# A selective-scan layer: the products with C on GpSimd, half of the B scalings on ScalarE, state copies on VectorE

## The chip, the core and the metric

The kernel runs on one core of a Trainium2 chip. A core has five engines that run side by side, each in its own program order: TensorE (PE in the profile, with its weight loads as PEld), VectorE (DVE), ScalarE (ACT), GpSimd (POOL) and SyncE (SP), which issues most DMAs. Engines wait for each other by semaphores. [...] The metric is the device time of one execution in microseconds (us), lower being better: 5,275.88 us as the median of three runs (5,275.79 to 5,280.46).

## The reference

The network has four layers on a tensor of 2 x 256 x 48 x 48, that is 2 images of 2,304 tokens with 256 channels. Only layer 0 is touched here, a Mamba layer that runs once forward ("f") and once backward ("b") over the tokens. Its core, for each of 512 inner channels d and 16 states n, is

```
xs   = silu(causal_conv(xi) + conv_b)              # 4 taps
proj = xs @ xproj_w.T                              # 16 for dt, 16 for B, 16 for C
dt   = softplus(proj[:16] @ dtproj_w.T + dtproj_b)
A    = -exp(A_log)
h[t] = exp(dt[t] * A) * h[t-1] + (dt[t] * xs[t]) * B[t]     # scan over t
y[t] = sum over n of h[t] * C[t]  +  xs[t] * D
out  = x + ((y_f * silu(z) + y_b * silu(z)) @ out_proj_w.T)
```

The other layers (a convolution with linear attention, an attention with a routed feed-forward, and an attention with a mixture of experts) come after it and are the same in both kernels.

## The kernel before

Layer 0 is the function `layer0`. The tokens are cut into 6 chunks of W = 384, so with 2 images and 2 directions there are 24 pieces (`order`). A sequence is the 6 pieces of one image and direction; `step` is the chunk's number in it. All data is 32-bit floating point, with channels on the 128 partitions, so 512 inner channels make DB = 4 blocks, and a chunk makes TB = 3 blocks of 128 tokens.

A piece is a loop over 16 states n and, inside, 4 channel blocks d: 64 slots, called `TILES`, with slot number k. A slot handles one tile of 128 channels by 384 tokens:

- `decay` (L601): ScalarE computes he = exp(dt * A) for slot k + EXP_AHEAD (4), into one of 6 buffers.
- `scale_b` (L591): GpSimd multiplies dt * xs, which lies transposed (tokens on partitions, `dtt`), by the B of state n, one value per partition. There are three instructions of 128x512 for each state, two states ahead, into one of 3 `dbt` buffers.
- `turn_b` (L611): TensorE transposes these back into PSUM (`db`, 3 buffers), DB_AHEAD = 2 slots ahead.
- the scan (L744 forward, L746 backward): one VectorE instruction over the 384 tokens.
- the product with C (`cc`, broadcast over the partitions by DMA). For three states of four (`on_pool`) two scans write to SBUF (`ho`, 4 buffers), and GpSimd multiplies both at once (L753, 128x768, `hcp`, 7 buffers). For the fourth state (n % 4 == 3, slots 12 to 15, 28 to 31, 44 to 47, 60 to 63) the scan writes over `db` in PSUM, and VectorE multiplies (L760, 128x384, `hc`).
- the state after the chunk's last token, which starts the scan of the next piece, is copied by ScalarE (L755 for a pair, L762 for one) in all but the last piece of a sequence.
- `add_state` (L637): TensorE transposes the product and adds it up in PSUM over the states (`y`), POOL_LAG (10) or DVE_LAG (2) slots later, from the list `later`.

Between these, each slot leaves TensorE room for about one more matmul. `advance` fills it from generators, by how far each lags behind its line: `prepare` makes the next piece's inputs (convolution L319, x products L338, dt products L355, softplus, the dt-u product on GpSimd L377, its transposes L387) and is to be done by slot READY = 54; `project_in`, `project_out` and parts of later layers share the other way. Each way has one PSUM bank, which ScalarE or VectorE must empty before TensorE's next step. `begin` opens a piece's `y` in slots 8 to 10, `end` empties the last piece's in slot 7. SBUF buffers come from pools by tag; the layers are recorded through a scheduler that sets waits and may move instructions of an engine past others that are not ready.

Of the kernel before, what the change touches and what calls it, by code (L numbers as in the profile page):

```python
# [18 lines left out]
F32 = mybir.dt.float32  # L19
# [144 lines left out]
def layer0(ctx, E):  # L164
# [7 lines left out]
    EXP_AHEAD, DB_AHEAD, POOL_LAG, DVE_LAG = 4, 2, 10, 2  # L172
# [105 lines left out]
    for s in "fb":  # L278
        w_x[s] = big.tile([P, DB, 48], F32, name=f"w_x{s}")
        nc.sync.dma_start(w_x[s], p[f"xproj_wT_{s}"].rearrange("(k p) m -> p k m", p=P))  # L280
        w_dt[s] = big.tile([16, 512], F32, name=f"w_dt{s}")
        nc.sync.dma_start(w_dt[s], p[f"dtproj_wT_{s}"])
        nega[s] = big.tile([P, DB * NS], F32, name=f"nega{s}")
        nc.scalar.activation(nega[s], E.v(f"A_log_{s}"), AF.Exp)
        nc.vector.tensor_scalar(nega[s], nega[s], -1.0, None, ALU.mult)

        w_d[s] = big.tile([P, DB, P], F32, name=f"w_d{s}")
        for d in range(DB):
            nc.vector.tensor_scalar(w_d[s][:, d, :], E.ident, E.v(f"D_{s}", d, 1), None, ALU.mult)
# [15 lines left out]
    def prepare(b, s, step, c, got):  # L305
# [37 lines left out]
        pr = wp.tile([48, W], F32, tag="pr", name="pr")  # L343
        nc.scalar.copy(pr, pj[:48, :])
# [7 lines left out]
        bt = wp.tile([P, TB, 48], F32, tag="bt", name="bt")  # L352
# [12 lines left out]
        nc.vector.tensor_copy(bt.rearrange("p j n -> p (j n)"), pb[:, : TB * 48])  # L365
# [12 lines left out]
        yield 0  # L378
        yield 0
        yield 0  # L380
        yield 0
        yield 0
# [10 lines left out]
    N_PREPARE = 43  # L393
# [191 lines left out]
    def scale_b(g, j):  # L585

        if g * DB < last:
            pc, n, _ = at_piece(g * DB)
            if j == 0:
                dbt[g] = wp.tile([P, TB, D], F32, tag="dbt", name="dbt", bufs=3)  # L590
            nc.gpsimd.tensor_scalar(  # L591
                dbt[g][:, j, :], pc["dtt"][:, j, :], pc["bt"][:, j, 16 + n : 17 + n], 1.0,
                ALU.mult, ALU.mult,
            )
# [99 lines left out]
    for i in range(len(order)):  # L694
# [26 lines left out]
        if i + 1 < len(order):  # L721
            ways[0].append([prepare(*order[i + 1], made), N_PREPARE, 20 if i == 0 else 0, READY, 0])
        for n in range(NS):
            g = i * NS + n
            on_pool = n % 4 != 3
# [3 lines left out]
            for d in range(DB):  # L729
# [19 lines left out]
                end_at = W - 1 if fwd else 0  # L749
                if on_pool:  # L750
                    if d % 2:
                        hc = wp.tile([P, 2, W], F32, tag="hcp", name="hcp", bufs=7)
                        nc.gpsimd.tensor_tensor(hc, ho, bc(cc, [P, 2, W], 1), ALU.mult)  # L753
                        if step < NCH - 1:
                            nc.scalar.copy(state[:, n, d - 1 : d + 1], ho[:, :, end_at])  # L755
                        for e in range(2):
                            later.append((k + POOL_LAG + e, add_state, (pc, d - 1 + e, hc[:, e, :])))
                else:
                    hc = wp.tile([P, W], F32, tag="hc", name="hc", bufs=3)
                    nc.vector.tensor_tensor(hc, to, cc, ALU.mult)  # L760
                    if step < NCH - 1:
                        nc.scalar.copy(state[:, n, d : d + 1], to[:, end_at : end_at + 1])  # L762
                    later.append((k + DVE_LAG, add_state, (pc, d, hc)))
# [10 lines left out]
        later.append((k0 + TILES + 7, end, (pc,)))  # L774
# [1529 lines left out]
```

## Time and profile before

| what | value |
|---|---|
| timed median of three | 5,275.88 us |
| the profiled execution's own time | 5,228.29 us |
| its span, first to last instruction | 5,226.4 us |
| PE busy | 4,808.4 us, 92% |
| VectorE busy | 3,288.2 us, 63% |
| ScalarE busy | 2,406.3 us, 46% |
| GpSimd busy | 2,435.5 us, 47% |
| granted TensorE clock | 0.968 |

An engine's busy time is the sum of its instructions' spans. TensorE's matmuls overlap, so that its busy share is too high as a measure of use. The page cuts the span into 40 equal slices of 131 us; the Mamba layer is the part in which GpSimd is busy. A group of instructions is named by its source line, engine and operation, then what it writes and reads, then the count; after the bar come its busy time in us, the mean of one in ns, and the idle time of the engine just before such instructions with what ended it. A view of stretches gives the same busy times for any interval.

### The profile page before, as it was taken

Reading aid. Unit: us, or ns where it says so; the run is one execution under the profiler, and the core shown is the slowest. Engines: PE = TensorE matmul, PEld = TensorE weight load, DVE = VectorE, ACT = ScalarE, POOL = GpSimd, SP = SyncE. Lnnn points to the kernel's source line nnn. Section 1 sums busy time; section 2 is a strip of 40 time slices with the busy share of each in tenths; the row PEclk is TensorE's granted clock in tenths of the full one; section 3 lists DMA queues with packets and bytes.
Section 4 is the critical chain, followed back from the end, with each engine's and each line's share of the span. In section 5 each row is a group of like instructions: output and inputs, shape, how many; then the busy total and the mean of one; then the engine's idle time right before and its main releaser. Section 6 shows DMA issues by size and latency. Waiting matters only on the chain. (4 is left out here: it accounts for less than half of the span.)

```text
span 5226.4 us, 61396 instructions
## 1 busy us (share of the span) xinstructions
PE 4808.4 (92%) x22242; PEld 3138.2 (60%) x22242; DVE 3288.2 (63%) x4801; ACT 2406.3 (46%) x4600; POOL 2435.5 (47%) x2091
## 2 busy tenths in 40 slices
PE   7888899899899889888999999999999999999897
PEld 4666666666666666665555555556655555555675
DVE  4888888888887878888999445456725400212344
ACT  5767767776667667662223223322133222222221
POOL 4798888888898888883000000048512100000321
PEclk8999999999999999999999999999989999999999
DMA  3222222222211122213110000111121100000423
GB/s 98 79 74 78 81 78 87 89 84 83 83 63 56 55 70 86 77 61 112 39 45 29 7 16 1 42 34 28 16 97 49 49 6 6 7 10 9 85 83 99
DMA packets 156377, 294.16 MB, mean 56 GB/s; under 512 B 29495, under 2 KB 108347, under 8 KB 155804
## 3 DMA queue, kind: packets, MB, share of 16 engines
q1 hardware_dynamic: 147356, 277.37, 15.5%
q0 software_dynamic: 8704, 12.73, 1.6%
q8 instruction: 179, 2.93, 0.2%
q14 instruction: 138, 1.13, 0.1%
HBM read 211.97 MB, written 78.07 MB: 55 GB/s over the span
## 5 line engine op out<-in xcount | busy, mean ns | idle before, releaser
L753 POOL TENSOR_TENSOR hcp<-ho,cc 128x768 f32<-128x768 f32 x576 | 1078.6, 1874 | 175.4 <-DVE ho L744 88.1
L591 POOL TENSOR_SCALAR dbt<-dtt,bt 128x512 f32<-128x512 f32 x1152 | 860.1, 764 | 147.1 <-PE db L611 141.8
L611 PE MATMUL db<-ident,dbt 128*128 128x128 f32 x4608 | 794.8, 283 | 101.3 <-DVE ho L744 32.1
L611 PEld LDWEIGHTS db<-ident,dbt 128*128 128x128 f32 x4608 | 565.0, 144 | 463.9 <-issue 187.4
L637 PE MATMUL y<-ident,hcp 128*128 128x128 f32 x3456 | 577.4, 276 | 6.1 <-POOL hcp L753 6.1
L601 ACT ACTIVATE he<-dt,negab 128x384 f32<-128x384 f32 x768 | 461.4, 613 | 186.1 <-DVE ho L746 108.0
L601 ACT ACTIVATE he<-dt,negaf 128x384 f32<-128x384 f32 x768 | 463.3, 614 | 177.0 <-DVE ho L744 124.1
L744 DVE TENSOR_TENSOR_SCAN ho<-he,state,db 128x384 f32<-128x384 f32 x480 | 464.9, 1002 | 121.2 <-PE db L611 108.2
L746 DVE TENSOR_TENSOR_SCAN ho<-he,state,db 128x384 f32<-128x384 f32 x480 | 467.9, 1002 | 110.8 <-PE db L611 94.8
L637 PEld LDWEIGHTS y<-ident,hcp 128*128 128x128 f32 x3456 | 421.3, 143 | 29.9 <-issue 20.9
L2107 POOL DMA_INDIRECT xe<-xt_d,token x48 | 47.5, 990 | 753.9 <-issue 713.2
L319 PE MATMUL mm<-xw,w_cv 128*128 128x384 f32 x768 | 312.7, 494 | 37.2 <-ACT xs L329 24.6
L2042 PE MATMUL po<-at,xtok 128*128 128x384 f32 x864 | 329.5, 506 | 8.2 <-ACT at L2040 8.1
L2040 ACT ACTIVATE at<-sp 128x384 f32<-128x384 f32 x216 | 104.8, 491 | 467.2 <-PE sp L2033 467.1
L2033 PE MATMUL sp<-qT,xn 128*128 128x384 f32 x864 | 317.2, 486 | 0.0
L1680 PE MATMUL ph<-xn,w 128*128 128x384 f32 x768 | 286.0, 515 | 17.7 <-ACT hid L1684 7.0
L1238 POOL PARTITION_ALL_REDUCE most<-most x1 | 0.4, 422 | 621.0 <-DVE most L1237 621.0
L969 PE MATMUL pf<-t,wfc 128*128 128x384 f32 x768 | 254.9, 487 | 3.0 <-ACT hid L973 2.9
L2042 PEld LDWEIGHTS po<-at,xtok 128*128 128x128 f32 x864 | 149.8, 189 | 177.4 <-ACT at L2040 108.4
L988 PE MATMUL po<-hid,wfc 128*128 128x384 f32 x768 | 253.6, 486 | 0.0
L1684 ACT ACTIVATE hid<-ph,vec 128x384 f32<-128x384 f32 x192 | 110.6, 581 | 290.2 <-PE ph L1680 256.6
L2033 PEld LDWEIGHTS sp<-qT,xn 128*128 128x128 f32 x864 | 161.6, 190 | 105.2
(481 smaller groups left out, 8791.0 us busy)
## 6 DMA issues: line engine op xcount, KB each, us to landing
cc<-bcd SPq DMA_DIRECT2D x96, 768.0 KB, 4.0
xw<-xi_d SPq DMA_DIRECT2D x24, 774.0 KB, 4.6
w<-in_m_w SPq DMA_DIRECT2D x16, 1024.0 KB, 5.5
y_d<-y SPq DMA_DIRECT2D x32, 384.0 KB, 2.3
ye<-y_d SPq DMA_DIRECT2D x32, 384.0 KB, 3.1
xi_d<-xz SPq DMA_DIRECT2D x48, 192.0 KB, 1.9
z_d<-xz SPq DMA_DIRECT2D x36, 256.0 KB, 2.3
y<-z_d SPq DMA_DIRECT2D x12, 768.0 KB, 4.1
```

The costliest lines, as they stand in the source:

```text
L319: nc.tensor.matmul(px, lhsT=w_cv[b, s][:, d * 4 + k, :], rhs=xw[:, d, o : o + W], start=k == 0, stop=k == 3,)
L591: nc.gpsimd.tensor_scalar(dbt[g][:, j, :], pc["dtt"][:, j, :], pc["bt"][:, j, 16 + n : 17 + n], 1.0, ALU.mult, ALU.mult,)
L601: nc.scalar.activation(hes[k], pc["dt"][:, d, :], AF.Exp, scale=nega[pc["s"]][:, d * NS + n : d * NS + n + 1])
L611: nc.tensor.transpose(dbs[k][:, j * P : (j + 1) * P], dbt[k // DB][:, j, d * P : (d + 1) * P], E.ident)
L637: nc.tensor.matmul(pc["yt"][j][:, d * P : (d + 1) * P], lhsT=hc[:, j * P : (j + 1) * P], rhs=E.ident, is_transpose=True, start=False, stop ...
L744: nc.vector.tensor_tensor_scan(to, he, db, init, ALU.mult, ALU.add)
L746: nc.vector.tensor_tensor_scan(to[:, ::-1], he[:, ::-1], db[:, ::-1], init, ALU.mult, ALU.add)
L753: nc.gpsimd.tensor_tensor(hc, ho, bc(cc, [P, 2, W], 1), ALU.mult)
L969: nc.tensor.matmul(pf, lhsT=wfc1[:, k, f * P : (f + 1) * P], rhs=t1[:, k, :], start=k == 0, stop=k == 1,)
L1680: nc.tensor.matmul(ph, lhsT=w1[:, e, k, f * P : (f + 1) * P], rhs=xn[:, k, c * W : (c + 1) * W], start=k == 0, stop=k == 1,)
L2033: nc.tensor.matmul(sp, lhsT=xn[:, k, t0 + i * P : t0 + (i + 1) * P], rhs=qT[:, k, c * W : (c + 1) * W], start=k == 0, stop=k == 1,)
L2042: nc.tensor.matmul(po[m], lhsT=xtok[:, i, m * P : (m + 1) * P], rhs=at, start=i == 0, stop=i == MT - 1,)
```

## The change

- Every state's scans go in pairs to `ho`, and every product with C is made by GpSimd, 128x768; the VectorE path and its buffers are gone, with one LAG of 10.
- Of the three scalings by B of a state, ScalarE makes the first, and for odd n the second too; GpSimd makes the rest.
- The state is copied by VectorE, two blocks at a time.
- Exps go 6 ahead in place of 4, with 8 buffers in place of 6.
- The weights of the x products and dt products are widened with zeros or neighbouring columns, so that these matmuls use all 128 rows and columns; the transposes of the projection are then 128 wide, and only the 16 columns of B are copied out.
- `prepare` is to be done by slot 48, with 8 empty steps in place of 5 between the dt-u product and its transposes; `begin`, `end` and `project_out` move by some slots.

```diff
-    EXP_AHEAD, DB_AHEAD, POOL_LAG, DVE_LAG = 4, 2, 10, 2
+    NX = 3 * NS
+    EXP_AHEAD, DB_AHEAD, LAG = 6, 2, 10
...
-        w_x[s] = big.tile([P, DB, 48], F32, name=f"w_x{s}")
+        w_x[s] = big.tile([P, DB * NX + P - NX], F32, name=f"w_x{s}")
+        nc.vector.memset(w_x[s][:, DB * NX :], 0.0)
...
-        w_dt[s] = big.tile([16, 512], F32, name=f"w_dt{s}")
-        nc.sync.dma_start(w_dt[s], p[f"dtproj_wT_{s}"])
+        w_dt[s] = big.tile([P, D], F32, name=f"w_dt{s}")
+        nc.vector.memset(w_dt[s], 0.0)
+        nc.sync.dma_start(w_dt[s][0:NS, :], p[f"dtproj_wT_{s}"])
...
-                pj[:48, :], lhsT=w_x[s][:, d, :], rhs=xs[:, d, :], start=d == 0, stop=d == DB - 1
+                pj, lhsT=w_x[s][:, d * NX : d * NX + P], rhs=xs[:, d, :], start=d == 0, stop=d == DB - 1
...
-                pd, lhsT=w_dt[s][:, d * P : (d + 1) * P], rhs=pr[0:16, :], start=True, stop=True
+                pd, lhsT=w_dt[s][:, d * P : (d + 1) * P], rhs=pr, start=True, stop=True
...
-            nc.tensor.transpose(pb[:, j * 48 : (j + 1) * 48], pr[:, j * P : (j + 1) * P], E.ident[0:48, 0:48])
-        nc.vector.tensor_copy(bt.rearrange("p j n -> p (j n)"), pb[:, : TB * 48])
+            nc.tensor.transpose(pb[:, j * P : (j + 1) * P], pr[:, j * P : (j + 1) * P], E.ident)
+        nc.vector.tensor_copy(bt, pb.rearrange("p (j n) -> p j n", j=DB)[:, :TB, NS : 2 * NS])
...
-        yield 0
-        yield 0
-        yield 0
-        yield 0
-        yield 0
+        for _ in range(8):
+            yield 0
...
-    N_PREPARE = 43
+    N_PREPARE = 46
...
-            nc.gpsimd.tensor_scalar(
-                dbt[g][:, j, :], pc["dtt"][:, j, :], pc["bt"][:, j, 16 + n : 17 + n], 1.0,
-                ALU.mult, ALU.mult,
-            )
+            to, at, b_n = dbt[g][:, j, :], pc["dtt"][:, j, :], pc["bt"][:, j, n : n + 1]
+            if j == 0 or j == 1 and n % 2:
+                nc.scalar.activation(to, at, AF.Copy, scale=b_n)
+            else:
+                nc.gpsimd.tensor_scalar(to, at, b_n, 1.0, ALU.mult, ALU.mult)
...
-            hes[k] = wp.tile([P, W], F32, tag="he", name="he", bufs=6)
+            hes[k] = wp.tile([P, W], F32, tag="he", name="he", bufs=8)
...
-            later.append((k0 + 8 + j, begin, (pc, j)))
+            later.append((k0 + LAG + 1 + j, begin, (pc, j)))
...
-        at = 8
+        at = LAG + 1
         if after:
-            ways[1].append([after, N_OUT, at, at + 18, 0])
-            at += 19
+            ways[1].append([after, N_OUT, at, at + 12, 0])
+            at += 13
...
-            ways[0].append([prepare(*order[i + 1], made), N_PREPARE, 20 if i == 0 else 0, READY, 0])
+            ways[0].append([prepare(*order[i + 1], made), N_PREPARE, 20 if i == 0 else 0, READY - 6, 0])
...
-                if on_pool:
-                    if d % 2 == 0:
-                        ho = wp.tile([P, 2, W], F32, tag="ho", name="ho", bufs=4)
-                    to = ho[:, d % 2, :]
-                else:
-                    to = db
+                if d % 2 == 0:
+                    ho = wp.tile([P, 2, W], F32, tag="ho", name="ho", bufs=4)
+                to = ho[:, d % 2, :]
...
-                        if step < NCH - 1:
-                            nc.scalar.copy(state[:, n, d - 1 : d + 1], ho[:, :, end_at])
-                        for e in range(2):
-                            later.append((k + POOL_LAG + e, add_state, (pc, d - 1 + e, hc[:, e, :])))
-                else:
-                    hc = wp.tile([P, W], F32, tag="hc", name="hc", bufs=3)
-                    nc.vector.tensor_tensor(hc, to, cc, ALU.mult)
+                if d % 2:
+                    hc = wp.tile([P, 2, W], F32, tag="hcp", name="hcp", bufs=7)
+                    nc.gpsimd.tensor_tensor(hc, ho, bc(cc, [P, 2, W], 1), ALU.mult)
                     if step < NCH - 1:
-                        nc.scalar.copy(state[:, n, d : d + 1], to[:, end_at : end_at + 1])
-                    later.append((k + DVE_LAG, add_state, (pc, d, hc)))
+                        nc.vector.tensor_copy(state[:, n, d - 1 : d + 1], ho[:, :, W - 1 if fwd else 0])
+                    for e in range(2):
+                        later.append((max(k + e, k0 + 3) + LAG, add_state, (pc, d - 1 + e, hc[:, e, :])))
...
-        later.append((k0 + TILES + 7, end, (pc,)))
+        later.append((k0 + TILES + LAG + 1, end, (pc,)))
```

More of the change, by code (lines that the diff above doesn't have):

```diff
@@ L278, in layer0 @@
     for s in "fb":
-        w_x[s] = big.tile([P, DB, 48], F32, name=f"w_x{s}")
-        nc.sync.dma_start(w_x[s], p[f"xproj_wT_{s}"].rearrange("(k p) m -> p k m", p=P))
-        w_dt[s] = big.tile([16, 512], F32, name=f"w_dt{s}")
-        nc.sync.dma_start(w_dt[s], p[f"dtproj_wT_{s}"])
+        w_x[s] = big.tile([P, DB * NX + P - NX], F32, name=f"w_x{s}")
+        nc.vector.memset(w_x[s][:, DB * NX :], 0.0)
+        nc.sync.dma_start(
+            w_x[s][:, : DB * NX].rearrange("p (k m) -> p k m", k=DB),
+            p[f"xproj_wT_{s}"].rearrange("(k p) m -> p k m", p=P),
+        )
+        w_dt[s] = big.tile([P, D], F32, name=f"w_dt{s}")
+        nc.vector.memset(w_dt[s], 0.0)
+        nc.sync.dma_start(w_dt[s][0:NS, :], p[f"dtproj_wT_{s}"])
         nega[s] = big.tile([P, DB * NS], F32, name=f"nega{s}")
@@ L342, in prepare @@
                 yield 1
-        pr = wp.tile([48, W], F32, tag="pr", name="pr")
-        nc.scalar.copy(pr, pj[:48, :])
+        pr = wp.tile([P, W], F32, tag="pr", name="pr")
+        nc.scalar.copy(pr, pj)
         bcd = dr.tile([NS, W], F32, tag="bcd", name="bcd")
@@ L351, in prepare @@
         ex = up.tile([P, DB, W], F32, tag="ex", name="ex")
-        bt = wp.tile([P, TB, 48], F32, tag="bt", name="bt")
+        bt = wp.tile([P, TB, NS], F32, tag="bt", name="bt")
         for d in range(DB):
@@ L721, in layer0 @@
         if i + 1 < len(order):
-            ways[0].append([prepare(*order[i + 1], made), N_PREPARE, 20 if i == 0 else 0, READY, 0])
+            ways[0].append([prepare(*order[i + 1], made), N_PREPARE, 20 if i == 0 else 0, READY - 6, 0])
         for n in range(NS):
             g = i * NS + n
-            on_pool = n % 4 != 3
             if n % 4 == 0:
@@ L748, in layer0 @@
                     )
[L749 to L753, printed above, removed]
-                        if step < NCH - 1:
-                            nc.scalar.copy(state[:, n, d - 1 : d + 1], ho[:, :, end_at])
-                        for e in range(2):
-                            later.append((k + POOL_LAG + e, add_state, (pc, d - 1 + e, hc[:, e, :])))
-                else:
-                    hc = wp.tile([P, W], F32, tag="hc", name="hc", bufs=3)
-                    nc.vector.tensor_tensor(hc, to, cc, ALU.mult)
+                if d % 2:
+                    hc = wp.tile([P, 2, W], F32, tag="hcp", name="hcp", bufs=7)
+                    nc.gpsimd.tensor_tensor(hc, ho, bc(cc, [P, 2, W], 1), ALU.mult)
                     if step < NCH - 1:
-                        nc.scalar.copy(state[:, n, d : d + 1], to[:, end_at : end_at + 1])
-                    later.append((k + DVE_LAG, add_state, (pc, d, hc)))
+                        nc.vector.tensor_copy(state[:, n, d - 1 : d + 1], ho[:, :, W - 1 if fwd else 0])
+                    for e in range(2):
+                        later.append((max(k + e, k0 + 3) + LAG, add_state, (pc, d - 1 + e, hc[:, e, :])))
                 later.sort(key=lambda e: e[0])
```

## The prediction

> **What bounds the kernel now.** I read the page's slices first: GpSimd (POOL) is busy only in the first 19 of 40, so the Mamba layer, the only thing that changes, is the first 2,402 us. Then that stretch, from the first scan to the last, in the view of stretches (columns: length, then busy us of PE, PEld, DVE, ACT, POOL, then granted clock, DMA share, GB/s):
>
> ```profile
> 79.20:2402.00 2322.80, 2055.64 (x12465) 1502.93 (x12464) 1921.42 (x2196) 1612.71 (x3261) 1982.62 (x1749) 0.97 0.22 76
> ```
>
> It holds 24 pieces of 64 slots (one scan each), 96.8 us a piece. No engine is alone at its limit: VectorE is idle 401 us, GpSimd 340, ScalarE 710. PE's 2,056 overstates it, since its pipelined rows overlap. So I cut one ordinary piece at its scans 0, 8, 32, 40, 48 and 64 and read the same columns:
>
> ```profile
> 1632.10:1641.90 9.80, 9.80 (x65) 7.61 (x66) 7.83 (x10) 5.31 (x14) 9.80 (x11) 1.00 0.19 80
> 1641.90:1678.70 36.80, 34.67 (x211) 24.78 (x210) 27.57 (x32) 26.15 (x58) 31.76 (x32) 1.00 0.22 77
> 1678.70:1691.60 12.90, 12.85 (x79) 8.72 (x77) 8.36 (x10) 12.09 (x28) 9.12 (x9) 1.00 0.16 61
> 1691.60:1711.50 19.90, 15.07 (x65) 9.44 (x65) 16.46 (x17) 15.92 (x36) 18.19 (x12) 0.83 0.08 21
> 1711.50:1728.30 16.80, 14.26 (x115) 12.23 (x114) 16.75 (x23) 11.96 (x29) 14.85 (x14) 1.00 0.13 48
> ```
>
> The first stretch fills GpSimd; the middle two fill PE, with ScalarE at 94% in slots 32-40; slots 40-48 hold the end of the next piece's preparation, PE half idle and its clock at 0.83; the last 16 slots fill VectorE (16.75 of 16.80). An instruction more on VectorE costs time there, and is hidden in the middle. The rows that the change touches (line, engine, operation, count | busy us, mean ns | idle before, releaser):
>
> ```profile
> L760 DVE TENSOR_TENSOR hc<-db,cc 128x384 f32<-128x384 f32 x384 | 202.1, 545 | 6.2 <-PE y L637 2.0
> L755 ACT COPY state<-ho 128x2 f32<-128x2 f32 x480 | 91.3, 190 | 183.5 <-DVE ho L746 100.5 <-DVE ho L744 79.3 <-DVE ub L467 1.1
> L753 POOL TENSOR_TENSOR hcp<-ho,cc 128x768 f32<-128x768 f32 x576 | 1078.6, 1874 | 175.4 <-DVE ho L744 88.1 <-DVE ho L746 84.3 <-PE db L611 1.6
> L591 POOL TENSOR_SCALAR dbt<-dtt,bt 128x512 f32<-128x512 f32 x1152 | 860.1, 764 | 147.1 <-PE db L611 141.8 <-ACT dtt L388 2.4 <-ACT state L762 1.5
> L387 PE MATMUL mm<-ident,dtu 128*128 128x128 f32 x288 | 61.5, 354 | 59.8 <-POOL dtu L377 59.7
> ```
>
> What decides is how a small VectorE instruction fares beside a running GpSimd one. VectorE's and GpSimd's lines of the timeline (start, length):
>
> ```profile
> 1377.29 1.81 POOL L753 TENSOR_TENSOR hcp<-ho,cc 128x768 f32<-128x768 f32 x1
> 1377.98 1.14 DVE L485 TENSOR_TENSOR off<-gn 128x2 f32<-128x2 f32 x1
> 1379.07 0.70 POOL L591 TENSOR_SCALAR dbt<-dtt,bt 128x512 f32<-128x512 f32 x1
> 1379.15 0.64 DVE L486 TENSOR_SCALAR off<-off 128x2 f32<-128x2 f32 x1
> ...
> 1408.69 1.04 DVE L468 TENSOR_TENSOR ub<-ub,vec 128x1 f32<-128x1 f32 x1
> ```
>
> L485 moves two elements and lasts until 1379.12, where the product of 1377.29 ends (1379.10); L486, one SBUF source and an SBUF target like the new state copy, ends at 1379.79 with the GpSimd instruction beside it (1379.77). Each waited for the other engine's instruction to end. And GpSimd is seldom free when a pair of scans ends:
>
> ```profile
> POOL hcp L753 <- DVE ho L744: 88.1, 52, 4.2
> POOL hcp L753 <- DVE ho L746: 84.3, 47, 3.8
> ```
>
> Only 99 of its 576 products had to wait for the scan; for the other 83% it was still at something else.
>
> **The change part by part.** One profiled execution took 5,228.3 us (span 5,226.4 and 1.9 around it); the timed median is 5,275.9, 47.6 above it. I sum against the profiled one and add the difference to the median.
>
> **1. C products.** VectorE loses 384 products of 545 ns: 202 us, 16 a piece, 4 in each of slots 12-15, 28-31, 44-47 and 60-63. GpSimd gains 192 of 1,874 ns (360 us) and loses half of its 1,152 B scalings of 764 ns (440 us): 80 us less. Per piece that is 32 x 1.874 + 24 x 0.764 + 3.4 for the dt-u product = 81.7 us of 96.8.
>
> [...]
>
> **2. State copies.** 640 copies of 128x2 (32 a piece, in the 20 pieces that are not a sequence's last) go from ScalarE to VectorE, SBUF to SBUF. Each stands behind the scan whose end it waits for, with the next scan behind it; turn_b on PE, only two tiles ahead, waits for that scan. Bounds for one: 0.16 us with no wait (a 128x2 copy from PSUM takes 159 ns, L143) and 2.03 if a whole product of 1.87 goes first. I take 0.70, between L486 (0.64) and the mean of the six L468 (707 ns, 134 at the least), the nearest rows. By stretch:
> - slots 0-8: 4 x 0.70 = 2.8, VectorE's idle time 1.97: 0.8 on the path, x 20 = **+16**.
> - slots 48-64: 8 x 0.70 - 4 x 0.545 = 3.4, idle 0.05: 3.4 x 20 = **+68**; the 4 last pieces only lose products, -2.2 each: **-9**. GpSimd says the same: 8 x 1.874 + 6 x 0.764 + 8 x 0.16 = 20.9 us in a stretch of 16.8.
> - slots 8-48: 20 x 0.70 - 12 x 0.545 = 7.5, idle 9.2 + 4.5 + 3.4 = 17.1. Hidden by VectorE's waits for PE in the mean, but a late scan stalls PE when the two tiles are used up: a tenth of the 14 us shows, 1.4 x 20 = **+28**; none of it or all the 7.5 are the ends.
>
> [...]
>
> **3. B scalings on ScalarE.** 576 of 128x512 with a per-partition scale. Nearest rows: 575 ns (L266, a 128x512 copy from PSUM) and, from the form with such a scale, 391 ns at 128 columns (L302) and 614 at 384 (L601), which gives 725 at 512; I take 725, 418 us, against 138 us of state copies that go (91.3 + 46.7, L755 and L762). ScalarE goes from 1,613 to 1,893 us: hidden by its idle 710 except in slots 32-40: 3 x 0.725 - 4 x 0.19 = 1.4 against 0.8 idle: 0.6 x 24 = **+14** (0 to 34). Exps run 6 ahead in place of 4 and he has 8 buffers, so scans are covered; what queues behind a scaling is the emptying of PE's one bank per way, priced among the rivals.
>
> **4. The dt-u product.** PE waits 59.7 us for it (2.5 a piece). Three more slots stand between GpSimd's multiply and its transposes, some 4 us, but GpSimd now carries products of slots 44-47 that it did not have. Half goes, **-30** (0 to -60); what is late next is the same instruction behind those products.
>
> **5. Waits for state copies on ScalarE.** PE waits 16.9 (L611) and 9.4 (L319) for L762, VectorE 7.1 for L755: 33 us; half shows, **-17**.
>
> **6. Padding.** A dt product with 16 rows holds PE 0.84 us (1301.28 to 1302.12), an x product with 48 columns 0.77 (799.17 to 799.94), a full one 0.65 (800.98 to 801.63): 96 x 0.19 + 96 x 0.12 = 30 us, less 72 transposes at 283 for 234 ns, 4 us. Half is in PE-bound slots, **-13** (0 to -26).
>
> **7. Rest.** The zeroing of four weights is in the first 80 us beside DMA; prepare, project_out and end shift by some slots with the same work; no DMA is added, and prepare's few (xw lands in 4.6 us) go out on SP a little sooner. The last products of the layer now come from GpSimd ten slots late: one piece's tail, **+5**.
>
> Sum: 16 + 68 - 9 + 28 + 14 - 30 - 17 - 13 + 5 = **+62 us**: 5,290 profiled, **5,338** timed, 1.2% slower.
>
> **The rivals.**
> - *The copies slip in between (faster).* The copy and GpSimd's next product wait for the same scan, and the copy need not cross engines; where GpSimd has caught up it costs 0.16. For it: 17% of products already wait for the scan, and GpSimd has 80 us less to do. Against: 83%. Then slots 0-8 and 8-48 cost nothing, slots 48-64 give -18 - 9, and with the rest unchanged the sum is -68: 5,208; with items 4 to 6 in full -127: 5,149. The sign turns where the mean copy costs 0.47.
> - *The product wins.* Both are released together; if half the copies wait for a whole product the mean is 1.16: 53 + 142 - 9 + 84 (a quarter of the middle's 16.7) + 14 - 60 + 5 = +229: 5,505. For it: L468's longest, 1.09. Against: GpSimd then falls idle and catches up.
> - *ScalarE becomes the bound* of slots 8-48 (54.2 us busy of 69.6, plus 7.3): six emptyings a piece late by a scaling, 6 x 0.725 x 24 = +104 on top: 5,442. Against: its waits for state copies go.
> - *All is hidden,* about 5,276.
>
> **How the numbers follow.** This kernel's measurement can tell 0.2%, 10.6 us. My forecast's case (5,290 to 5,440) gets 0.43, the copies that slip in 0.28, the product first 0.13, ScalarE 0.07, no change 0.09. Slower 0.63, same 0.09, faster 0.28. The range reaches from 5,200 (a third of the faster case lies below) to 5,500 (the worst of the second rival above); the likeliest case's own is 5,290 to 5,440.
>
> **What would show it.** Right: the new state copies on VectorE at a mean near 0.7 us, ending with a GpSimd instruction; slots 48-64 near 20 us; the wait before the dt-u transposes halved. Wrong: copies near 0.16 us, or PE waiting for ScalarE more than for VectorE. The forecast fails most easily on the copies' mean, 4 us of the kernel for each 0.02.

## The result and the profile after

The changed kernel takes **5,348.6 us** (median of 4 runs, 5,346.5 to 5,351.6); the kernel before took 5,278.2 beside it (4 runs, 5,275.8 to 5,282.1). The ratio is **1.0133** with a 95% interval of 1.0116 to 1.0151: slower by 70 us, 61 to 80 by the interval. The forecast was 5,338 and +62.

Where the time sits. In the trace of before the scans of piece 1 start at 79.2 us and those of piece 24 at 2,305.5; after, at 81.5 and 2,376.6. The Mamba layer accounts for 71 us, all of the timed difference. (The profiled run of before was 47.6 us under its timed median. What follows the first scan of piece 24, mostly layers that no edit touches, took 2,921 us there and 2,973 in the profile after; so I compare the Mamba layer's landmarks, not the spans.)

The view of stretches of after, from the first scan to the end of the last piece (columns: length, busy us of PE, PEld, DVE, ACT, POOL, granted clock, DMA share, GB/s):

```profile
81.50:2473.00 2391.50, 2056.11 (x12474) 1536.23 (x12472) 2053.50 (x2458) 1853.42 (x3041) 1925.24 (x1367) 0.96 0.22 74
```

Before, the same work took 2,323 us. VectorE is up from 1,921 to 2,054 although 202 us of products were taken from it; GpSimd is down by 57 and ScalarE up by 241. The costliest groups on the page, for the lines that the change touched (out<-in, count | busy us, mean ns | idle before, releaser):

```profile
L751 POOL TENSOR_TENSOR hcp<-ho,cc 128x768 f32<-128x768 f32 x768 | 1424.1, 1860 | 356.7 <-DVE ho L746 141.0
...
L598 POOL TENSOR_SCALAR dbt<-dtt,bt 128x512 f32<-128x512 f32 x576 | 435.8, 765 | 61.2 <-PE db L615 52.2
L596 ACT ACTIVATE dbt<-dtt,bt 128x512 f32<-128x512 f32 x576 | 407.9, 711 | 8.2 <-PE db L615 8.0
...
L753 DVE COPY state<-ho 128x2 f32<-128x2 f32 x640 | 358.0, 559 | 17.1
```

The state copies of two elements a partition hold VectorE for 358 us, 559 ns each: more than the products that left. The mean hides two kinds. Of the 640 records, 336 last 0.3 us or less (57 us in all), 286 between 0.3 and 2 us (247 us), and 18 more than 2 us (53 us). Each of the 304 longer ones ends within 0.15 us of the end of a GpSimd instruction. VectorE's timeline shows both kinds in the last stretch of an ordinary piece, and two of the longest (start, length):

```profile
684.11 7.27 DVE L753 COPY state<-ho 128x2 f32<-128x2 f32 x1
...
868.77 3.38 DVE L753 COPY state<-ho 128x2 f32<-128x2 f32 x1
...
1775.26 0.17 DVE L753 COPY state<-ho 128x2 f32<-128x2 f32 x1
1775.37 1.92 DVE L744 TENSOR_TENSOR_SCAN ho<-he,state,db 128x384 f32<-128x384 f32 x2
1777.32 0.56 DVE L753 COPY state<-ho 128x2 f32<-128x2 f32 x1
1777.78 1.90 DVE L744 TENSOR_TENSOR_SCAN ho<-he,state,db 128x384 f32<-128x384 f32 x2
1779.72 0.17 DVE L753 COPY state<-ho 128x2 f32<-128x2 f32 x1
```

GpSimd's at the same times:

```profile
682.19 3.64 POOL L751 TENSOR_TENSOR hcp<-ho,cc 128x768 f32<-128x768 f32 x2
685.77 1.40 POOL L598 TENSOR_SCALAR dbt<-dtt,bt 128x512 f32<-128x512 f32 x2
687.09 3.60 POOL L751 TENSOR_TENSOR hcp<-ho,cc 128x768 f32<-128x768 f32 x2
690.63 0.73 POOL L598 TENSOR_SCALAR dbt<-dtt,bt 128x512 f32<-128x512 f32 x1
...
868.13 3.99 POOL L383 TENSOR_TENSOR dtu<-dt,xs 128x1536 f32<-128x1536 f32 x1 [3.67 <-DVE dt L381]
...
1775.36 1.82 POOL L751 TENSOR_TENSOR hcp<-ho,cc 128x768 f32<-128x768 f32 x1 [1.07 <-ACT he L605]
1777.16 0.69 POOL L598 TENSOR_SCALAR dbt<-dtt,bt 128x512 f32<-128x512 f32 x1
1777.82 1.81 POOL L751 TENSOR_TENSOR hcp<-ho,cc 128x768 f32<-128x768 f32 x1
1779.83 1.82 POOL L751 TENSOR_TENSOR hcp<-ho,cc 128x768 f32<-128x768 f32 x1 [0.20 <-PE y L641]
```

At 1775.26 GpSimd is idle; the copy takes 0.17 us and GpSimd's next product starts 0.10 us behind its start. At 1777.32 a scaling has been running since 1777.16; the copy ends at 1777.88, the scaling at 1777.85. At 684.11 GpSimd works without a gap: the copy ends at 691.38, with the scaling that ends at 691.36; besides the product that was running, two scalings, two products and one more scaling went first. So a waiting copy need not be next in line. But that is rare: in the trace 296 of the 304 longer copies end with the GpSimd instruction that was running when they began (4 times, that began with them), 7 were passed by one more product and 1 by five instructions. Of the 18 over 2 us, 10 were passed by nothing: they ended with the running dt-u product, GpSimd's longest instruction there (3.42 to 4.00 us), as the copy of 868.77 does (872.15 and 872.12).

PE's waits, in the stretch that the prediction used (79.2 to 2,402 us, which here ends some 71 us before the layer does), as who waited for whom: us in total, times, longest. First the waits for scans before:

```profile
PE db L611 <- DVE ho L744: 32.1, 55, 3.3
PE db L611 <- DVE ho L746: 19.9, 48, 2.3
```

and the largest waits after:

```profile
PE db L615 <- DVE ho L744: 79.1, 121, 2.0
PE mm L390 <- POOL dtu L383: 58.9, 21, 7.9
PE db L615 <- DVE ho L746: 53.5, 70, 6.2
PE mm L325 <- ACT xs L335: 46.2, 48, 4.1
```

PE waits for scans 132.6 us (the B transposes, two tiles ahead, write into the buffer that an earlier scan frees); before it was 52.0. The wait for the dt-u product, which the forecast halved, is as it was. And GpSimd's products with C wait for scans more often than before, 272 times in this stretch, which holds 746 of the 768 products, where it was 99 of 576:

```profile
POOL hcp L751 <- DVE ho L746: 139.1, 142, 4.3
POOL hcp L751 <- DVE ho L744: 125.1, 130, 4.3
```

One ordinary piece of after, cut at its scans 0, 8, 32, 40, 48 and 64 (the view of stretches, columns as above):

```profile
1696.03:1706.32 10.29, 8.98 (x54) 6.40 (x54) 9.31 (x13) 7.69 (x15) 10.10 (x10) 1.00 0.23 78
1706.32:1742.87 36.55, 34.98 (x218) 26.30 (x217) 26.80 (x36) 29.14 (x51) 27.59 (x22) 1.00 0.23 78
1742.87:1760.59 17.72, 14.92 (x94) 10.66 (x92) 16.29 (x17) 17.62 (x29) 15.55 (x8) 1.00 0.12 45
1760.59:1772.02 11.43, 8.74 (x43) 6.89 (x44) 10.63 (x13) 6.22 (x12) 10.35 (x8) 0.70 0.00 0
1772.02:1791.63 19.61, 17.75 (x122) 13.10 (x121) 19.33 (x27) 15.76 (x31) 18.14 (x14) 1.00 0.19 61
```

The last stretch is VectorE's again (19.33 of 19.61), now with copies in place of products. In slots 32 to 40 ScalarE is at 17.62 of 17.72: the end of the next piece's preparation now falls there, and less of it in slots 40 to 48. One piece is not the mean; over the 20 pieces that copy states, from the starts of the scans in the traces (us):

| slots | before | after | after, copies on ScalarE (below) |
|---|---|---|---|
| 0-8 | 8.4 | 11.3 | 10.0 |
| 8-32 | 36.3 | 36.6 | 35.8 |
| 32-40 | 12.2 | 15.0 | 14.6 |
| 40-48 | 17.9 | 12.9 | 11.3 |
| 48-64 | 22.0 | 25.6 | 22.1 |
| piece | 96.8 | 101.3 | 93.8 |

### The profile page after: what moved, and what is told of

It reads as the page before. It is cut to its first block, busy times and chain, and to the rows that moved or that the text cites. A ratio compares the mean times of both kernels' runs of the same rounds, so it can differ in the third digit from the quotient of the medians.

```text
span 5349.7 us, 60998 instructions
## 1 busy us (share of the span) xinstructions
PE 4825.7 (90%) x22242; PEld 3177.4 (59%) x22242; DVE 3420.2 (64%) x5061; ACT 2645.9 (49%) x4379; POOL 2370.2 (44%) x1707
## 5 line engine op out<-in xcount | busy, mean ns | idle before, releaser
L751 POOL TENSOR_TENSOR hcp<-ho,cc 128x768 f32<-128x768 f32 x768 | 1424.1, 1860 | 356.7 <-DVE ho L746 141.0
L615 PE MATMUL db<-ident,dbt 128*128 128x128 f32 x4608 | 811.7, 284 | 153.9 <-DVE ho L744 79.1
L641 PE MATMUL y<-ident,hcp 128*128 128x128 f32 x4608 | 749.0, 277 | 7.5 <-POOL hcp L751 7.4
L746 DVE TENSOR_TENSOR_SCAN ho<-he,state,db 128x384 f32<-128x384 f32 x640 | 625.8, 1002 | 122.2 <-PE db L615 96.7
L744 DVE TENSOR_TENSOR_SCAN ho<-he,state,db 128x384 f32<-128x384 f32 x640 | 622.4, 1000 | 115.1 <-PE db L615 81.7
L641 PEld LDWEIGHTS y<-ident,hcp 128*128 128x128 f32 x4608 | 563.5, 143 | 43.0 <-issue 26.7
L605 ACT ACTIVATE he<-dt,negab 128x384 f32<-128x384 f32 x768 | 448.9, 610 | 215.5 <-DVE ho L746 211.6
L605 ACT ACTIVATE he<-dt,negaf 128x384 f32<-128x384 f32 x768 | 451.3, 611 | 172.1 <-DVE ho L744 164.4
L598 POOL TENSOR_SCALAR dbt<-dtt,bt 128x512 f32<-128x512 f32 x576 | 435.8, 765 | 61.2 <-PE db L615 52.2
L596 ACT ACTIVATE dbt<-dtt,bt 128x512 f32<-128x512 f32 x576 | 407.9, 711 | 8.2 <-PE db L615 8.0
L753 DVE COPY state<-ho 128x2 f32<-128x2 f32 x640 | 358.0, 559 | 17.1
L325 PE MATMUL mm<-xw,w_cv 128*128 128x384 f32 x768 | 323.3, 510 | 50.2 <-ACT xs L335 46.2
```

The lines of the kernel that those rows point to most:

```text
L596: nc.scalar.activation(to, at, AF.Copy, scale=b_n)
L598: nc.gpsimd.tensor_scalar(to, at, b_n, 1.0, ALU.mult, ALU.mult)
L605: nc.scalar.activation(hes[k], pc["dt"][:, d, :], AF.Exp, scale=nega[pc["s"]][:, d * NS + n : d * NS + n + 1])
L615: nc.tensor.transpose(dbs[k][:, j * P : (j + 1) * P], dbt[k // DB][:, j, d * P : (d + 1) * P], E.ident)
L641: nc.tensor.matmul(pc["yt"][j][:, d * P : (d + 1) * P], lhsT=hc[:, j * P : (j + 1) * P], rhs=E.ident, is_transpose=True, start=False, stop ...
L744: nc.vector.tensor_tensor_scan(to, he, db, init, ALU.mult, ALU.add)
```

## The experiments

My theory: the copies alone turn a gain into a loss, because a two-element copy waits for GpSimd's instruction to end. The rivals: the load on VectorE or GpSimd as such, the products with C, ScalarE's new scalings. Each run's ratio is to the kernel before on the same chip; before took 5,234 to 5,237 us there, or 5,281 on the chip of the fifth to eighth, so 0.001 is 5.2 to 5.3 us. The difference between the chips lies in what no edit touches: from the first scan of piece 24 to the last instruction the profiles have 2,966 to 2,975 us on the chip of the fifth to eighth and 2,921 to 2,930 on the others.

**1. The copies on ScalarE, all else as in after.**

```diff
-    nc.vector.tensor_copy(state[:, n, d - 1 : d + 1], ho[:, :, W - 1 if fwd else 0])
+    nc.scalar.copy(state[:, n, d - 1 : d + 1], ho[:, :, W - 1 if fwd else 0])
```

> The changed kernel with its 640 state copies back on ScalarE (nothing else undone). Theory A, the copies' waits for GpSimd instructions are the loss: VectorE sheds the 358 us that its copies took, the pieces with copies (95 to 108 us in the changed kernel) come near the pieces without (88.5 to 97), some 6 us each, 20 pieces: 5,160 to 5,260 us, below the kernel before (5,278). Theory B, the loss is in the products and scalings that moved (GpSimd and ScalarE too full): 5,320 to 5,350, as the changed kernel.

Measured: 5,153.4 us, ratio 0.9836 (0.9818 to 0.9853); of the 5,278 us that theory A was set against, that is 5,192. The rest of the change gains 1.64%, 86 us; the one line that moves the copies costs 0.0297, some 157 us. On ScalarE the same 640 copies take 187 ns each. Their row among the groups of ScalarE:

```profile
L753 ACT COPY state<-ho 128x2 f32<-128x2 f32 x640 | 119.4, 187 | 72.2 <-DVE ho L746 40.6 <-DVE ho L744 28.3 <-DVE ub L471 0.6
```

**2. The copy as a reduction over one element, on VectorE.** Same engine, same bytes, same place in the order; another instruction.

```diff
-    nc.vector.tensor_copy(state[:, n, d - 1 : d + 1], ho[:, :, W - 1 if fwd else 0])
+    at_end = W - 1 if fwd else 0
+    nc.vector.tensor_reduce(
+        state[:, n, d - 1 : d + 1], ho[:, :, at_end : at_end + 1], AX.X, ALU.max
+    )
```

> The changed kernel with the copies still on VectorE, same elements at the same places, but as a maximum over one element in place of a copy. Theory A, and the wait comes with the copy's form: each takes 0.15 to 0.2 us with no long ones, 640 x 0.17 = 109 us in place of 358, and the time is that of the copies on ScalarE or a little less: 5,150 to 5,260. Theory A, and any VectorE instruction from SBUF to SBUF waits: mean near 0.56 us, 5,330 to 5,360. Theory B: 5,320 to 5,350 with short instructions.

Measured: 5,169.9 us, 0.9874 (0.9857 to 0.9891). The view of the tile (duration ns least/median/most):

```profile
L754 DVE TENSOR_REDUCE state<-ho x640: 118/155/159, 82.0 to 2237.5; 128x2 f32<-128x2 f32 x160
```

Not one of 640 waits. So it isn't VectorE as the place, nor the order; it is what kind of instruction the copy is.

**3. No copies.** This kernel leaves the carry of the state from piece to piece out (the state stays zero).

```diff
+    nc.vector.memset(state, 0.0)
...
-                    if step < NCH - 1:
-                        nc.vector.tensor_copy(state[:, n, d - 1 : d + 1], ho[:, :, W - 1 if fwd else 0])
```

> The changed kernel without the state copies: the state is zero at every piece's start, so the carry from piece to piece is left out. It bounds what any placement of the copies can win. Theory A: all pieces near 88.5 to 97 us, 5,130 to 5,240. Theory B: 5,310 to 5,350.

Measured: 5,161.7 us, 0.9856 (0.984 to 0.9873), the same as with the copies on ScalarE within the intervals. On ScalarE the copies cost nothing that shows; as a reduction on VectorE (0.9874) they cost some 0.2%, about what the intervals leave open. Against no copies at all, those of the change cost 0.0277, some 146 us.

**4. Before, with both of its copies on VectorE.** The one edit alone, in the old arrangement, with the products with C still shared and GpSimd making all scalings.

```diff
-    nc.scalar.copy(state[:, n, d - 1 : d + 1], ho[:, :, end_at])
+    nc.vector.tensor_copy(state[:, n, d - 1 : d + 1], ho[:, :, end_at])
...
-    nc.scalar.copy(state[:, n, d : d + 1], to[:, end_at : end_at + 1])
+    nc.vector.tensor_copy(state[:, n, d : d + 1], to[:, end_at : end_at + 1])
```

> The kernel before with its state copies moved to VectorE and nothing else changed: 480 of 128x2 from SBUF, 320 of 128x1 from PSUM. Theory A: the 480 wait as in the changed kernel (GpSimd is still at something else for 83% of its products), mean 0.5 to 0.7 us, the 320 take 0.16; 60 to 130 us slower, 5,340 to 5,410. Theory B: 5,265 to 5,290.

Measured: 5,392.9 us, 1.0301 (1.0282 to 1.0319), +156 us, more than the 60 to 130 expected; the 480 pairs have a mean of 665 ns. The view of the tile:

```profile
L755 DVE COPY state<-ho x480: 135/486/6005, 83.3 to 2455.9; 128x2 f32<-128x2 f32 x160
...
L762 DVE COPY state<-db x320: 136/145/153, 100.6 to 2462.0; 128x1 f32<-128x1 f32 x160
```

Moving the copies costs as much here (0.0301) as at the end of the change (0.0297): the loss comes with this move, whether or not the other edits are made. The 480 pairs from SBUF take up to 6.0 us; the 320 single ones, whose source is in PSUM, never wait (153 ns at most). This run can't tell whether that is for the source or for the one element; the next one can.

**5. Two single copies in place of one of two elements,** from SBUF as in after.

```diff
-    nc.vector.tensor_copy(state[:, n, d - 1 : d + 1], ho[:, :, W - 1 if fwd else 0])
+    end_at = W - 1 if fwd else 0
+    for e in range(2):
+        nc.vector.tensor_copy(
+            state[:, n, d - 1 + e : d + e], ho[:, e, end_at : end_at + 1]
+        )
```

> The changed kernel with each state copy of two elements a partition cut into two copies of one element (1,280 of 128x1). If only a copy of two or more elements waits for GpSimd: each 0.14 us like the copies from PSUM (145 ns), 180 us on VectorE in place of 358, ratio to the kernel before 0.985 to 1.000. If any copy from SBUF to SBUF waits: at least one of the two waits as the one did, 0.56 + 0.15 or more for the pair, ratio 1.01 to 1.06.

Measured: 5,232.5 us, 0.9908 (0.9891 to 0.9926).

```profile
L755 DVE COPY state<-ho x1280: 118/153/158, 82.6 to 2260.3; 128x1 f32<-128x1 f32 x183
```

Twice the copies, twice the issues, and none waits: 185 us of VectorE in place of 358, and 0.0225 of the ratio, 119 us, comes back. So among these copies the number of elements decides, with the source in SBUF both times; the reduction of experiment 2 moves two elements and doesn't wait either, so the kind of instruction counts too. What in the core makes the one kind wait and the other not, no run shows. The three forms also show how dear VectorE's time is, against the copies on ScalarE: 96 us of reductions cost 0.0038 (20 us), 185 us of single copies 0.0072 (38 us), about a fifth; 358 us of waiting copies cost 157, 44%. Waiting time was dearer here than plain work. A likely reason, which no run tests alone, is that it comes in pieces longer than the two tiles of cover can take; the copies over 2 us hold only 53 of the 358 us.

**6. All B scalings on GpSimd,** as before, on top of experiment 1.

```diff
-            if j == 0 or j == 1 and n % 2:
-                nc.scalar.activation(to, at, AF.Copy, scale=b_n)
-            else:
-                nc.gpsimd.tensor_scalar(to, at, b_n, 1.0, ALU.mult, ALU.mult)
+            nc.gpsimd.tensor_scalar(to, at, b_n, 1.0, ALU.mult, ALU.mult)
```

> The changed kernel with the copies on ScalarE and with all 1,152 B scalings on GpSimd: its load is 32 x 1.86 + 48 x 0.765 + 3.4 = 99.7 us a piece plus what VectorE's large additions hold up, where pieces took 85 to 105. Theory A (the scalings on ScalarE pay for the products on GpSimd): GpSimd becomes the bound, 103 to 108 us a piece, ratio 1.04 to 1.09. Theory B (ScalarE's scalings cost as much as they free): 0.98 to 1.00.

Measured: 5,372.1 us, 1.0174 (1.0157 to 1.0191): 0.0338 (178 us) worse than experiment 1, though less than the 4 to 9% over before that I had expected. The stretch, columns as above:

```profile
79.00:2400.00 2321.00, 1975.87 (x12042) 1501.54 (x12042) 1740.21 (x1737) 1565.56 (x3051) 2231.66 (x1876) 0.95 0.22 73
```

GpSimd is busy for 96% of it and is the bound. All products with C fit on GpSimd only because ScalarE takes half of the scalings; the two edits belong together.

**7. No padding,** on top of experiment 1: x products 48 wide, dt products and B transposes as before.

```diff
-                pj, lhsT=w_x[s][:, d * NX : d * NX + P], rhs=xs[:, d, :], start=d == 0, stop=d == DB - 1
+                pj[:NX, :], lhsT=w_x[s][:, d * NX : (d + 1) * NX], rhs=xs[:, d, :], start=d == 0, stop=d == DB - 1
...
-                pd, lhsT=w_dt[s][:, d * P : (d + 1) * P], rhs=pr, start=True, stop=True
+                pd, lhsT=w_dt[s][:, d * P : (d + 1) * P], rhs=pr[0:NS, :], start=True, stop=True
```

> The changed kernel with the copies on ScalarE and the weights of the x and dt products unpadded (48 columns, 16 rows). The forecast gave the padding 13 us (0 to 26): ratio 0.984 + 0.0025 = 0.9865 (0.984 to 0.989). The mean durations of the traces (dt products 541 to 522 ns, x products 498 to 498) give 4 us: 0.984 to 0.985.

Measured: 5,236.7 us, 0.991 (0.9894 to 0.9927). Padding is worth 0.0074, 39 us, three times the forecast's 13. The stretch from the first scan to the end of the layer, first with padding (experiment 1):

```profile
83.40:2318.00 2234.60, 1999.84 (x12466) 1516.58 (x12465) 1738.52 (x1810) 1892.24 (x3681) 1928.49 (x1367) 0.97 0.24 78
```

and without:

```profile
83.50:2360.00 2276.50, 2053.75 (x12462) 1510.93 (x12461) 1740.99 (x1810) 1896.88 (x3681) 1930.41 (x1367) 0.96 0.23 76
```

With as many matmuls, PE is busy 54 us longer without padding, while VectorE, ScalarE and GpSimd do the same work in the same time. The granted clock goes with it: 0.969 over the run with padding, 0.961 without (both in the profiled run). The two runs were on different chips, and before has 0.966 on the one and 0.963 on the other as the mean of its runs; but over the scans of pieces 1 to 23 alone, by the clock records of the traces, it is 0.971 with padding and still 0.961 without. Matmuls that the padding does not touch are longer too (B transposes 283 for 278 ns, dt-u transposes 351 for 322, in the groups of PE between 84 and 2,100 us).

**8. Six more empty steps before the dt-u transposes,** and the preparation's end four slots later, on top of experiment 1.

```diff
-        for _ in range(8):
+        for _ in range(14):
...
-    N_PREPARE = 46
+    N_PREPARE = 52
...
-            ways[0].append([prepare(*order[i + 1], made), N_PREPARE, 20 if i == 0 else 0, READY - 6, 0])
+            ways[0].append([prepare(*order[i + 1], made), N_PREPARE, 20 if i == 0 else 0, READY - 2, 0])
```

> The changed kernel with the copies on ScalarE and 14 in place of 8 empty steps between the dt-u product and its transposes, prepare paced to slot 52. If PE's wait for that product (58.6 us there) only lacks slots: the wait falls below 25 us and the granted clock rises, ratio 0.970 to 0.980. If GpSimd and VectorE fall behind by as much whatever the slots: the wait stays at 45 to 60 us, 0.982 to 0.988.

Measured: 5,181.5 us, 0.9812 (0.9795 to 0.9828), 0.0024 (13 us) under experiment 1, with intervals that just overlap. PE's wait for the product:

```profile
PE mm L390 <- POOL dtu L383: 57.7, 19, 8.8
```

The wait stays as it was (58.6 us in experiment 1), as the second theory says. What little is won is won elsewhere: in the traces the first scan of piece 24 comes at 2,207 us in place of 2,229.

**9. A quarter of the products with C back on VectorE,** on top of experiment 1 (every fourth state, with 384 products, single copies on ScalarE; the decays go 5 ahead in 7 buffers in place of 6 ahead in 8).

```diff
+                on_pool = n % 4 != 3
...
+                else:
+                    hc = wp.tile([P, W], F32, tag="hc", name="hc", bufs=3)
+                    nc.vector.tensor_tensor(hc, to, cc, ALU.mult)
+                    if step < NCH - 1:
+                        at_end = W - 1 if fwd else 0
+                        nc.scalar.copy(state[:, n, d : d + 1], to[:, at_end : at_end + 1])
+                    later.append((k + 2, add_state, (pc, d, hc)))
```

> The version with the state copies on ScalarE (0.9836 of before), with the products with C of every fourth block back on VectorE (384 products of 128x384, 202.1 us in before, 192 fewer GpSimd products of 1.86 us, 357 us), their single state copies on ScalarE, and the decays 5 ahead in 7 buffers, which the memory forces. Theory A: the 202 us on VectorE were on the path by about a quarter, as the forecast took them, so the ratio goes back by some 50 us, to 0.990 to 1.000. Theory B: VectorE has slack once the copies are gone (415 us before the scans with a carried state in the scalar-copy version), while GpSimd becomes free for other work, so the quarter costs nothing or gains: 0.975 to 0.986.

Measured: 5,210.4 us, 0.9954 (0.9938 to 0.9971): 0.0118, 62 us, worse. GpSimd's groups show that the time freed there bought nothing:

```profile
L756 POOL TENSOR_TENSOR hcp<-ho,cc 128x768 f32<-128x768 f32 x576 | 1053.8, 1837 | 429.3 <-DVE ho L748 207.6 <-DVE ho L750 151.4 <-ACT he L605 59.9
```

GpSimd loses some 350 us of products and idles instead, waiting for scans. Not all of the 62 us need be the 203 us on VectorE: PE here also waits 40.9 us for the single state copies on ScalarE, which hold the scan's PSUM bank, and the decays have a buffer less.

**10. Only the dt products back at 16 rows,** on top of experiment 1.

```diff
-        w_dt[s] = big.tile([P, D], F32, name=f"w_dt{s}")
-        nc.vector.memset(w_dt[s], 0.0)
-        nc.sync.dma_start(w_dt[s][0:NS, :], p[f"dtproj_wT_{s}"])
+        w_dt[s] = big.tile([NS, D], F32, name=f"w_dt{s}")
+        nc.sync.dma_start(w_dt[s], p[f"dtproj_wT_{s}"])
...
-                pd, lhsT=w_dt[s][:, d * P : (d + 1) * P], rhs=pr, start=True, stop=True
+                pd, lhsT=w_dt[s][:, d * P : (d + 1) * P], rhs=pr[0:NS, :], start=True, stop=True
```

> The version with the state copies on ScalarE (0.9836), with the dt products alone back at 16 rows; the B and C products and the transposes of B stay padded. Without any padding the ratio was 0.991, some 39 us more, and the granted clock of the run 0.961 instead of 0.969. Theory A: the loss comes from the few products themselves and is shared about evenly between the 96 dt products and the rest: 0.986 to 0.989, clock about 0.965. Theory B: the loss is a clock effect of the 16-row products, which use the fewest rows: nearly the whole of it comes back, 0.990 to 0.992, clock 0.961 to 0.963. Theory C: it comes from the 48-column products and the transposes of B: below 0.985, clock 0.968 to 0.970.

Measured: 5,170.0 us, 0.9875 (0.9858 to 0.9891), clock 0.965 in the profiled run, and 0.965 over the scans of pieces 1 to 23: half of the padding's worth (0.0039, 20 us) and some half of the clock's step in that stretch. The rest (0.0035) belongs to the x products and the B transposes. The clock moves along with the padded share in the three runs; whether the products change the clock, or a shorter idle in the layer does, these runs can't separate. Experiment 11 speaks for the second: it changes no matmul, yet has 0.979 over the same scans and dt-u transposes of 304 ns.

**11. The dt-u product on VectorE,** on top of experiment 1.

```diff
-        nc.gpsimd.tensor_tensor(dtu, dt, xs, ALU.mult)
+        nc.vector.tensor_tensor(dtu, dt, xs, ALU.mult)
```

> The version with the state copies on ScalarE (0.9836), with the 24 products dt times u moved from GpSimd (3.43 us each) to VectorE, right behind the two additions that feed them. Theory A: the wait of TensorE for this product, 58.6 us in 21 pieces, is the product's own time plus its place in GpSimd's queue, so on VectorE (about 1.9 to 2.5 us each by the rows of the additions, beside it) most of it goes: wait under 25 us, ratio 0.973 to 0.980. Theory B: the slot order, not the engine, leaves the transposes too early; the wait stays above 40 us and the ratio at 0.982 to 0.986, or rises by the 45 to 60 us added to VectorE.

Measured: 5,120.7 us, 0.9784 (0.9768 to 0.98), 0.0052 (27 us) better. PE's wait for the product, in experiment 1:

```profile
PE mm L390 <- POOL dtu L383: 58.6, 21, 7.6
```

and here:

```profile
PE mm L390 <- DVE dtu L383: 24.3, 8, 6.2
```

The wait falls from 58.6 us in 21 pieces to 24.3 in 8. Each product takes 1.93 us on VectorE for 3.53 on GpSimd. GpSimd's queue is not what the move saves: from the end of the subtraction that feeds it (L381) to its start a product waits 0.84 us in the mean on GpSimd (experiment 1) and 0.78 on VectorE. The shorter instruction alone is 1.60 us for each of 24 products, 38 us, and the wait fell by 34.

**12. Experiments 8 and 11 together.** The edits are the two above.

> The version with the state copies on ScalarE and the dt-u products on VectorE (0.9784 of before), with the six more empty steps between this product and its transposes (14 in place of 8) and the preparation ending four slots later. In the version that had the six steps alone the ratio was 0.9812 and the wait for the product 57.7 us, in the one with the product on VectorE alone 24.3 us in 8 pieces. Theory A: with the product out of GpSimd's queue the steps now give it time; the wait falls below 10 us and the ratio to 0.972 to 0.978. Theory B: the steps only move the transposes into the next piece's fuller slots and the wait of 24 us turns into others; 0.977 to 0.982.

Measured: 5,111.0 us against 5,237.0, ratio **0.9763** (0.975 to 0.9777). It is the fastest kernel here, 2.4% under the one before and some 3.7% under the changed one. Of what theory A said, the ratio came and the wait did not: PE still waits 28.1 us in 8 pieces for the product. The small step to experiment 11 (0.0021, 11 us) lies within the intervals; it is the second time that the steps gained about as much, and the wait for the product is not where.

## Why the prediction was right, and where it was not

The sign and the size were right: +62 forecast, +70 measured, on its likeliest case. The mechanism was right too; that the sum came so close is in part luck, since several terms were off and cancelled. Point by point:

- **What decides** (a small VectorE instruction beside a running GpSimd one): right. Experiments 1 and 4 show that this move alone is +157 us and +156, experiment 2 that the form of the copy is what waits, and experiment 1 that the other edits together gain 86. In the forecast's own terms, what would not have been paid without the copies is 16 + 68 - 9 + 28 = 103 plus the 52 us that the products free in the last stretch: 155. That is the sum's largest part, and it met the measured 157 (146 against no copies, experiment 3).
- **The mean of a copy**, 0.70: measured 0.559. The rival "the copies slip in" was in part right: 336 of 640 do. Its turning point was 0.47, and the measured mean lies above it. The forecast's rate, 4 us for 0.02, was too low by its own terms: 4 + 8 + 2 copies on the path in 20 pieces make 5.6 us for 0.02, and at 0.559 the sum would have been some +23. The missing part is that a copy showed more of its time on the path (44%) than the 35% of the working (155 of 448). Two errors of opposite sign; that they cancelled was luck. The bound of 2.03 us, "a whole product goes first", was passed by 18 copies: 10 met the dt-u product, 3.42 to 4.00 us, which the bound forgot, and 8 were passed by a further instruction. (In the rival "the product wins" the mean does not follow either: half of the copies at 2.03 and half at 0.16 give 1.10, not 1.16.)
- **Where the copies cost:** slots 0-8 +1.3 us a piece (after against experiment 1) for 0.8; slots 48-64 +3.5 for 5.6; slots 8-48 +2.7 for 1.4. Together 7.5 for 7.8. The middle hides less than I took.
- **"Slots 48-64 near 20 us":** wrong, 25.6. But experiment 1 has 22.1 there. I read the stretch from one piece of 16.8, while the mean of the 20 was 22.0; the stretch chosen as ordinary was a short one. In it VectorE was idle for 0.05 us; in the mean it was busy 89% of this stretch before, 97% after and 90% in experiment 1. The growth, 3.6 us, met the forecast's 3.4, but from two parts that were both off: the copies added 3.5 for 5.6, and the products that left took off nothing (22.0 before, 22.1 in experiment 1) for 2.2.
- **Item 1, products with C:** 52 us in the last stretch were my worth for it, and the last stretch does not show them. Experiment 9 gives 62 for the whole, with the two other causes named there, and there it is slots 40 to 48 that grow, 11.3 to 16.6 us, while slots 48 to 64 shrink, 22.1 to 20.5. So the size may be right and the place was wrong; how much of the 62 is the products, no run separates.
- **Item 3, ScalarE:** a scaling takes 711 ns for 725. The rival that ScalarE bounds the middle did not come: PE's wait for xs is 46.2 us in after, yet 23.0 with the copies on ScalarE, which has more to do there. That wait came with the copies. The +14 itself no run measures alone. What I did not say is that this edit is what makes item 1 possible (experiment 6, 178 us).
- **Item 4, the dt-u product, -30:** failed. The wait is 58.9 us for 59.7. It was not the "late next" that I named, the product behind products with C: in after it starts 0.76 us in the mean behind the subtraction that feeds it. Experiment 8 shows that six more steps leave the wait as it is, and experiment 11 that a faster engine for the product cuts it. Why the steps give it no time stays open.
- **Item 5, waits for state copies, -17:** not measured. The waits were mostly for the single copies from PSUM, and these are gone in after and in experiments 1 and 3 alike; the pairs on ScalarE cost nothing that shows (experiment 3 against 1). Experiment 9 brings the single copies back, with 40.9 us of waits, but other things with them.
- **Item 6, padding, -13 (0 to -26):** too small and outside its bounds; 39 us by experiment 7. I priced the rows of the padded products alone; others are shorter with them too, and why the runs leave open (experiment 10).

So items 4 and 6 came to -39 in place of -43, the copies to +157 in place of +155, and the waits, the scalings, the tail and the products can't be told apart from the re-pacing; all edits but the copies gained 86 where the forecast has 93. The total came out right through the copies, whose mechanism was right and whose price was right by two errors that cancelled.

## What to carry to other kernels

A VectorE copy of two elements beside a busy GpSimd can cost the rest of what GpSimd is doing (286 of 640 took 0.3 to 2 us here), not what it moves: give it to ScalarE (187 ns each in experiment 1), or write it as a form that didn't wait here (a reduction over one element, 159 ns at most; two single copies, 158 ns at most each), and read the spread of its durations, not the mean, to see it. When a change moves work to an engine until it fills, look for the small instruction that waits for that engine's instructions before counting what was saved (358 us of such copies here, against 202 us of products that left). When an engine waits for a product, compare how long the product waits to start with how long it runs before blaming a queue: here it was the run, 3.53 us against 1.93, and more steps of lead left the wait as it was.

## What the runs showed of the hardware that I had not expected

- A blocked two-element copy can be passed over: 8 of the 304 that waited were, 7 by one further product and one by five whole instructions that followed without a gap (7.27 us). The other 296 ended with the instruction that was running or began with them.
- Copies of one element a partition from SBUF (1,280, 118 to 158 ns) and a reduction over one element (640, 118 to 159 ns) never waited, beside the same GpSimd load. That is not so for every instruction on one element: the prediction's L468, a product with two inputs, took 1.04 us at 1408.69 and ended at 1409.73, with a GpSimd product that ended at 1409.72.
- With small matmuls widened to full rows and columns, other matmuls are shorter too: 54 us less of PE busy time in the Mamba layer for as many instructions (12,466 and 12,462), with a granted clock of 0.971 in place of 0.961 over the scans of pieces 1 to 23, and 0.965 with half of the widening. Whether the widening or the shorter waits raise the clock is open: moving the dt-u product to VectorE, which touches no matmul, raised it to 0.979 there (over the whole profiled run 0.972, for 0.969 in experiment 1).
